# Two preactivated 5x5 convolutions: loading rows once, moving boundary rows to GpSimd, and filtering seven more chunks in columns

## The chip, the core and the metric

The kernel runs on one core of a Trainium2 chip. The metric is the device time of one execution in microseconds (us); lower is better. Five engines work side by side, each through its own instruction queue in order: TensorE (PE in the profile, with its weight loads as PEld), VectorE (DVE), ScalarE (ACT), GpSimd (POOL) and SyncE (SP), which here only issues transfers. GpSimd and ScalarE issue a few transfers too.

## The reference

```python
# x: (8, 32, 252, 252) float32, two weights of (32, 32, 5, 5)
x = x + conv(group_norm(x), w0)   # layer 1: 16 groups of 2 channels, eps 1e-5
x = x + conv(group_norm(x), w1)   # layer 2
# conv: 5x5 over all 32 channels, reflect padding of 2, written in the reference by FFT
```

The output has the shape of `x`. In the code the layers are `l = 0` and `l = 1`; this text calls them layer 1 and layer 2.

## The kernel before, in words

**Layout.** The image is split by the parity of its columns and rows into four phases. A phase's 32 channels take a quarter of the 128 partitions, so that one matmul of 128x128 handles all phases and channels at once, and the 5x5 filter becomes 3x3 on a plane of 126x126. An image and layer are worked through in 8 chunks `c` of 16 plane rows (`ROWS`), which are 4 tiles (`NT`) of 4 rows.

**Row filtering.** In the rows the kernel uses a fast filtering scheme with six points: of six input rows each tile makes six combinations (points 2, 4, 1, 3, 0 and 5), each is multiplied with its own transformed weights, and the six products are combined to four output rows. `transform` makes the combinations on VectorE: `row_pairs` (differences of rows two apart, into tile `v`), `row_quads` (L571, L572) and `last_rows` (L578, L579), both into tile `u12`, then `point2` (L587), `point4` (L591), `point1` (L597), `point3` (L594) and `points05` (L604). In layer 2 the row sums come from two transfers on GpSimd's queue instead of `row_pairs`: `v<-y` (L552) copies the rows, and L554 and L555 add the rows two further down as they land. The last rows of a chunk need the first rows of the next chunk; `last_rows` is the part that reads them.

**Products.** `conv` multiplies (L680): three matmuls for each point, one for each column tap, of 504 columns in layer 1 and 508 in layer 2. An fp32 product appears as two records in the profile. Points 2 and 4 go to `m`, 1 and 3 to `pairs`, 0 and 5 to `sums05` or `extra`.

**Column filtering.** For some chunks points 0 and 5 are also filtered fast in the columns. `by_columns` names them. Then `points05` writes into the buffer of `u12`, `columns` makes differences of neighbouring columns (L613 to L623), and `column_product` (L702) does four products of half the width for each of the two points, where the plain form does three of full width. The two middle ones share a buffer `extra`: the first pair is multiplied, ScalarE copies half of it (`seed_columns`, L706) as the start value of the second pair, and TensorE adds the second pair to it. `column_parts` (L787 to L789) puts the parts together.

**ScalarE** seeds `pairs` from `m` (L724, L726), evacuates `m` to `sd` (L732) and the first pair to `sd` (L739), writes rows 0 and 3 of the output (L768, L780, L778), copies reflected borders of `y` (L864 to L867, L862), interleaves the phases for the store (L917), and sums an image's pixels for the statistics (L231, L237, L855).

**Input.** `load` brings a chunk of `x` into `xs` (two buffers) from SyncE's queue: four transfers of 504 KB, one for each phase. Since the two column parities of a row differ only by a shift of one column, two transfers are enough where `once` is true: `even_columns` then copies 64 partitions to the other 64 with ScalarE (L159). `borders` (L148 to L154) fills the reflected columns on GpSimd. `parts` says in which pieces of rows a chunk is loaded.

**Order.** The program order of every engine is written by hand: `at(t, fn, ...)` puts a call into a table with a planned time, and the calls are emitted in the order of these times. After the first image, layer 1 of image `b + 1` and layer 2 of image `b` alternate chunk by chunk. A step is the stretch in which TensorE works on one chunk's points 2, 4, 1 and 3; in it, `transform` prepares the next chunk, and the chunk before gets its points 0 and 5. `begin(i)` is the planned start of step `i`: 10.2 us for the four points, and 5.1 for plain or 3.4 for column-filtered points 0 and 5.

## Time and profile before

| | |
|---|---|
| time, median of 3 runs | 1892.61 us (1891.02 to 1893.24) |
| the profiled execution | 1893.14 us, of which the span of the trace is 1891.4 |
| TensorE | 1851.5 us busy, 98% of the span |
| VectorE | 1698.0 us, 90% |
| ScalarE | 1401.1 us, 74% |
| GpSimd | 372.9 us, 20% |
| mean granted TensorE clock | 0.994 of full speed |
| transfers | 411.41 MB, 218 GB/s |

The span runs from the first instruction to the last. Busy times are sums over the span, so an engine that is busy for 74% on average may be full in one stretch and idle in another. TensorE's busy time comes from modelled ends of pipelined matmuls. "A <- B" in a list of waits says that A's engine was idle before A until B was done.

The program has 128 steps, 77 of them column-filtered. The planned lengths are close to those in the trace: a column-filtered step of layer 1 followed by a plain one of layer 2 takes 13.56 and 11.94 us between first matmuls.

### The profile page before, as it was taken

Reading aid. Unit: us, or ns where it says so; the run is one execution under the profiler, and the core shown is the slowest. Engines: PE = TensorE matmul, PEld = TensorE weight load, DVE = VectorE, ACT = ScalarE, POOL = GpSimd, SP = SyncE. Lnnn points to the kernel's source line nnn. Section 1 sums busy time; section 2 is a strip of 40 time slices with the busy share of each in tenths; the row PEclk is TensorE's granted clock in tenths of the full one; section 3 lists DMA queues with packets and bytes.
Section 4 is the critical chain, followed back from the end, with each engine's and each line's share of the span. In section 5 each row is a group of like instructions: output and inputs, shape, how many; then the busy total and the mean of one; then the engine's idle time right before and its main releaser. Section 6 shows DMA issues by size and latency. Waiting matters only on the chain.

```text
span 1891.4 us, 20043 instructions
## 1 busy us (share of the span) xinstructions
PE 1851.5 (98%) x5162; PEld 956.7 (51%) x5162; DVE 1698.0 (90%) x2972; ACT 1401.1 (74%) x2695; POOL 372.9 (20%) x733
## 2 busy tenths in 40 slices
PE   5999999999999999999999999999999999999997
PEld 4444455545555555544555455555555545554455
DVE  7987899999998999999899898999989999998685
ACT  5887678778777787778787687877787765565665
POOL 4543211120112210131111310113111131111210
PEclk8999999999999999999999999999999999999999
DMA  9887899999999999999999989999999978995785
GB/s 278 205 176 191 201 248 230 212 229 253 219 239 239 206 249 233 212 244 219 246 224 229 220 214 258 221 227 226 215 260 220 236 184 177 193 203 145 192 217 113
DMA packets 248627, 411.41 MB, mean 218 GB/s; under 512 B 19520, under 2 KB 215488, under 8 KB 238144
## 3 DMA queue, kind: packets, MB, share of 16 engines
q1 hardware_dynamic: 220384, 272.09, 61.8%
q0 software_dynamic: 27648, 135.28, 28.7%
q10 hardware_dynamic: 480, 2.77, 0.4%
q8 instruction: 41, 0.67, 0.2%
q14 instruction: 74, 0.61, 0.1%
HBM read 207.41 MB, written 67.39 MB: 145 GB/s over the span
## 4 chain that ended last, share of the span: by engine, by line
PE 76%; DVE 9%; DMA 8%; ACT 3%; issue 2%; POOL 1%; SPq 0%; DVEq 0%; ACTq 0%; POOLq 0%
PE m L680 27%; PE pairs L680 26%; PE sums L680 8%; PE sums L702 6%; PE extra L702 6%; DMA v<-y 4%; PE extra L680 4%; DMA st<-in_x_dram 1%; DMA xs<-in_x_dram 1%; DMA out_dram<-o 1%; DVE sd L743 1%; ACT o L917 1%; DMA v<-ytail 1%; DVE t L604 1%; POOL u L479 0%
## 5 line engine op out<-in xcount | busy, mean ns | idle before, releaser
L680 PE MATMUL pairs<-t,u 128*128 128x504 f32 (+2 forms) x1548 | 690.4, 585 | 2.7 <-ACT pairs L726 1.6
L680 PE MATMUL m<-t,u 128*128 128x508 f32 (+3 forms) x1560 | 675.2, 581 | 7.1 <-DVE t L591 2.6
L680 PEld LDWEIGHTS m<-t,u 128*128 128x128 f32 x1560 | 293.3, 189 | 325.6 <-issue 297.4
L680 PEld LDWEIGHTS pairs<-t,u 128*128 128x128 f32 x1548 | 289.2, 189 | 321.5 <-issue 295.6
L917 ACT COPY o<-y 64x508 f32<-64x508 f32 x496 | 327.2, 660 | 8.9 <-DMA out_dram<-o 0.2
L743 DVE SCALAR_TENSOR_TENSOR sd<-sd,pairs 128x504 f32<-128x504 f32 (+2 forms) x258 | 163.9, 670 | 19.2 <-PE pairs L680 16.0
L680 PE MATMUL sums<-t,u 128*128 128x508 f32 (+5 forms) x408 | 175.3, 578 | 0.0
L855 ACT ACTIVATE junk<-y,negk 128x1008 bf16<-128x1008 f32 (+1 forms) x144 | 147.4, 1024 | 30.6 <-PE extra L702 14.9
L726 ACT COPY pairs<-m 128x504 f32<-128x504 f32 (+1 forms) x129 | 72.5, 562 | 129.6 <-PE m L680 110.0
L732 ACT COPY sd<-m 128x504 f32<-128x504 f32 (+2 forms) x258 | 137.0, 583 | 32.0 <-DVE sums L789 24.7
L604 DVE SCALAR_TENSOR_TENSOR t<-v 128x1024 f32<-128x1024 f32 (+1 forms) x128 | 157.5, 1230 | 3.5 <-PE sums L680 3.5
L702 PE MATMUL extra<-sdiff,wc 128*128 128x252 f32 (+3 forms) x616 | 156.3, 375 | 3.3 <-ACT extra L706 2.6
L702 PEld LDWEIGHTS extra<-sdiff,wc 128*128 128x128 f32 x616 | 113.5, 188 | 89.6 <-issue 50.2
L591 DVE SCALAR_TENSOR_TENSOR t<-v 128x512 f32<-128x512 f32 (+2 forms) x129 | 89.7, 695 | 65.6 <-DMA v<-y 47.7
L702 PE MATMUL sums<-d,u 128*128 128x252 f32 (+3 forms) x616 | 142.3, 373 | 0.0
L562 DVE TENSOR_TENSOR v<-xs 128x1792 f32<-128x1792 f32 (+1 forms) x65 | 129.5, 1993 | 1.8 <-issue 0.7
L554 POOL DMA_DIRECT2D v<-y x64 | 55.2, 863 | 377.7 <-DMA v<-y 377.7
L702 PEld LDWEIGHTS sums<-d,u 128*128 128x128 f32 x616 | 115.3, 189 | 26.9 <-issue 11.8
L237 ACT ACTIVATE st<-st,negk 128x1134 f32<-128x1134 f32 x98 | 121.7, 1242 | 3.2
L148 POOL COPY xs<-xs 64x32 f32<-64x32 f32 (+3 forms) x74 | 34.1, 461 | 450.2 <-DMA xs<-in_x_dram 330.7
L680 PEld LDWEIGHTS sums<-t,u 128*128 128x128 f32 x408 | 75.9, 188 | 80.1 <-issue 77.2
L231 ACT ACTIVATE st<-st 128x1134 f32<-128x1134 f32 x98 | 112.2, 1145 | 4.0 <-DMA st<-in_x_dram 2.8
(171 smaller groups left out, 2424.7 us busy)
## 6 DMA issues: line engine op xcount, KB each, us to landing
xs<-in_x_dram SPq DMA_DIRECT2D x176, 504.0 KB, 12.6
v<-y POOLq DMA_DIRECT2D x64, 1032.0 KB, 5.7
st<-in_x_dram SPq DMA_DIRECT2D x111, 567.0 KB, 6.9
out_dram<-o SPq DMA_DIRECT2D x488, 126.0 KB, 5.7
v<-y POOLq DMA_DIRECT2D x64, 903.0 KB, 9.9
u<-ud SPq DMA_DIRECT2D x15, 1152.0 KB, 5.6
xs<-in_x_dram SPq DMA_DIRECT2D x30, 441.0 KB, 6.7
xs<-in_x_dram SPq DMA_DIRECT2D x28, 472.5 KB, 11.1
```

The lines of the kernel that those rows point to most:

```text
L231: A.activation(junk, src, AF.Identity, accum_out=acc[:, 0, i : i + 1])
L237: A.activation(junk, src, AF.Square, bias=negk, accum_out=acc[:, 1, i : i + 1])
L562: V.tensor_sub(v[:, r0:r1], t[:, r0 + 2 : r1 + 2], t[:, r0:r1])
L591: stt(ts[b, l, c][0][:, 1, j0:j1], vt[:, :, 1], -2.0, vt[:, :, 2], ALU.mult, ALU.add)
L604: stt(t, got["vt"][:, :, 0:2], 4.0 if l else -4.0, got["vt"][:, :, 2:4], ALU.mult, ALU.add)
L680: T.matmul(dst, u[:, k, 2 - i, :], rhs[:, j0 + i0 : j0 + i1, i : i + wo], start=(i == 0 and not add), stop=(i == 2), skip_group_check=add,)
L702: T.matmul(dst[:, 0, use], w, rhs[:, use], start=(i == 2), stop=True, skip_group_check=(i != 2))
L726: A.copy(dst, src)
L732: A.copy(got["sd"][:, 1 + e], m24[e][:, 0:n])
L743: stt(d, d, -2.0, pairs13[e][:, 0:n], ALU.mult, ALU.add)
L855: A.activation(dst, src, AF.Square, bias=negk, scale=1.0 if i else -1.0, accum_out=acc[:, 1, at_ : at_ + 1])
L917: copy(got["o", h][halves[s], 0:m, cp::2], got["y"][halves[cp], r : r + m, :])
```

## The change

Rows of layer 1 are loaded once in more chunks: in image 1 in chunks 0 to 6 instead of 0 to 2, and in images 2 to 7 in chunks 0, 1 and 3 to 6 instead of none. That makes 40 more chunks with two transfers in place of four and with one ScalarE copy of 64x2048 elements. For them, and for the other chunks from (1,3) on, the planned times of load, borders and copy are new.

`last_rows` runs on GpSimd in all chunks but those of image 0 in layer 1. What was one VectorE instruction (scale and add) is there a scaling and an addition. Its planned time is 1.1 us earlier, except in layer 1 of the first two images.

`by_columns` names chunks 1, 3, 4, 6 and 7 of layer 2 for images 0 to 5 (before: 1, 3, 5 and 7) and 1, 3 and 4 for image 6 (before: 1 and 3).

```diff
     def once(b: int, c: int) -> bool:
 
-        return c < (NCH - 1, 3)[b] if b < 2 else False
+        return c < NCH - 1 and (b < 2 or c != 2)
 
     def parts(b: int, c: int):
 
         if once(b, c):
+            if b > 1 or (b == 1 and c > 2):
+                return ((0, ROWS),)
             return ((0, 10), (10, 6)) if (b, c) == (0, 0) else ((0, 2), (2, 14))
...
             u2, (t, nxt) = got["u"][:, 1], source()
+            eng = V if b + l == 0 else G
+            f = 4.0 if l else -4.0
+            if eng is V:
+                stt(u2[:, NT - 1], t[:, ROWS - 2], f, nxt[:, 0], ALU.mult, ALU.add)
+            else:
+                G.tensor_scalar(u2[:, NT - 1], t[:, ROWS - 2], f, None, ALU.mult)
+                G.tensor_add(u2[:, NT - 1], u2[:, NT - 1], nxt[:, 0])
             if l == 0:
-                V.tensor_sub(got["v"][:, ROWS - 2 : ROWS], nxt[:, 0:2], t[:, ROWS - 2 : ROWS])
-            stt(u2[:, NT - 1], t[:, ROWS - 2], 4.0 if l else -4.0, nxt[:, 0], ALU.mult, ALU.add)
+                eng.tensor_sub(got["v"][:, ROWS - 2 : ROWS], nxt[:, 0:2], t[:, ROWS - 2 : ROWS])
...
-            for dt, fn in ((2, row_quads), (3.2, last_rows), (3.6, point2)):
+            for dt, fn in ((2, row_quads), (3.2 if l == 0 and b < 2 else 2.1, last_rows), (3.6, point2)):
                 at(t0 + dt, fn)
...
-        return c in {B - 1: (1, 2, 4, 5), B - 2: (1, 3)}.get(b, (1, 3, 5, 7))
+        return c in {B - 1: (1, 2, 4, 5), B - 2: (1, 3, 4)}.get(b, (1, 3, 4, 6, 7))
...
                 for part in parts(*inputs[k]):
-                    early = once(*inputs[k]) or nb == 0
-                    at(t0 + (14.0 if nb == 0 and part[0] == ROWS else 4.0 if early else 9.5), load, *inputs[k], *part)
-                    at(t1 + (0.2 if early else 9.0), borders, *inputs[k], *part)
-                    if once(*inputs[k]):
-                        kb, kc = inputs[k]
-                        t = 5.25 if part[0] == 0 and (kb, kc) != (1, 0) else 13.55 if kb else 8.5
-                        at(t1 + t, even_columns, *inputs[k], *part)
+                    kb, kc = inputs[k]
+                    if kb > 1 or (kb == 1 and kc > 2):
+                        at(t0 + (7.5 if once(kb, kc) else 9.5), load, kb, kc, *part)
+                        at(t1 + (5.1 if once(kb, kc) else 9.0), borders, kb, kc, *part)
+                        if once(kb, kc):
+                            at(t1 + 6.3, even_columns, kb, kc, *part)
+                    else:
+                        early = once(kb, kc) or nb == 0
+                        at(t0 + (14.0 if nb == 0 and part[0] == ROWS else 4.0 if early else 9.5), load, kb, kc, *part)
+                        at(t1 + (0.2 if early else 9.0), borders, kb, kc, *part)
+                        if once(kb, kc):
+                            t = 5.25 if part[0] == 0 and (kb, kc) != (1, 0) else 13.55 if kb else 8.5
+                            at(t1 + t, even_columns, kb, kc, *part)
```

Here `V` is VectorE, `G` GpSimd, `stt` a VectorE instruction that scales one operand and adds another. In the last part `t0` and `t1` are the planned starts of the current and the next step, and `inputs[k]` is the chunk of `x` two ahead of the one that is transformed.

## The prediction
> **What bounds the kernel now.** The profiled execution took 1893.14 us around a span of 1891.4; the three timed runs have median 1892.61, 0.5 below it. I read the page's engine totals, then the chain of waits, then TensorE's own waits.

> ```profile
> PE 1851.5 (98%) x5162; PEld 956.7 (51%) x5162; DVE 1698.0 (90%) x2972; ACT 1401.1 (74%) x2695; POOL 372.9 (20%) x733
> ...
> PE 76%; DVE 9%; DMA 8%; ACT 3%; issue 2%; POOL 1%; SPq 0%; DVEq 0%; ACTq 0%; POOLq 0%
> ```

> ```profile
> PE extra L702 <- ACT extra L706: 2.6, 9, 0.9
> ```

> TensorE has work for 98% of the span, and outside the head hardly waits for anyone (last line: us in total, times, longest): a matmul less is time less, and a TensorE wait more is time more. The other engines matter only where they come late for a matmul. So I looked at one step in the timeline: the layer 1 step (4,0,3), filtered in columns, which starts at 929.85 (us from the span's start, us taken).

> ```profile
> 929.85 5.23 PE L680 MATMUL m<-t,u 128*128 128x504 f32 x12
> ...
> 932.45 0.64 ACT L780 ACTIVATE y<-sums 128x504 f32<-128x504 f32 x1
> ...
> 933.20 0.69 DVE L758 TENSOR_TENSOR sums<-pairs,sd 128x508 f32<-128x508 f32 x1
> ...
> 935.60 1.07 ACT L732 COPY sd<-m 128x504 f32<-128x504 f32 x2
> 935.72 1.21 DVE L617 TENSOR_TENSOR d<-t 128x1008 f32<-128x1008 f32 x1
> ...
> 936.96 0.70 DVE L571 SCALAR_TENSOR_TENSOR u<-y 128x516 f32<-128x516 f32 x1
> ...
> 937.71 0.58 ACT L739 COPY sd<-pairs 128x504 f32<-128x504 f32 x1 [1.04 <-PE pairs L680]
> ...
> 939.35 0.57 ACT L706 ACTIVATE extra<-extra 128x504 f32<-128x504 f32 x1 [0.36 <-PE extra L702]
> ...
> 940.84 1.01 PE L702 MATMUL extra<-sdiff,wc 128*128 128x252 f32 x4
> ```

> In times from the step's start: ScalarE ends the two evacuations (L732) at 6.8, and the seed L706 at 10.07; the second half of the middle column products (L702) needs that seed and starts at 10.99, 0.92 later. VectorE ends the last column difference (L617) at 7.08, and only then starts layer 2's next row filter (L571, 7.11). That is a floor: L758 starts at 3.35, just after ScalarE's L780 ends at 3.24 (it frees `sums05`), and ScalarE works without a gap from the evacuations of the step before to there. Over all column-filtered layer 1 steps in which a layer 2 chunk's rows are filtered, L571 starts between 7.09 and 9.88, never earlier.

> [...] at 805.62 a border copy (L154, else 0.21) took 1.22 beside a 1.24 us L604. [...] Here 128x384 takes GpSimd 1.255 (L459) and VectorE 0.566 (L572), 2.2 times.

> **The change part by part.**

> *Column filtering in seven more chunks.* Each drops six row products and adds eight half-width ones. From the chain (start, us):

> ```profile
> 941.86 5.11 PE sums L680 x12
> ...
> 956.35 1.70 PE pairs L680 x4
> 958.05 0.86 PE extra L702 x4
> 958.91 1.72 PE sums L702 x8
> ```

> 5.11 - (2 x 0.86 + 1.72) = 1.67 us, seven times: **-11.7 us** on the path. It costs VectorE seven more operations, 4.8 us a chunk (2.8 in the differences, 2.0 in the parts, 34 us in all), and ScalarE 0.7; the same chunks' neighbours lose theirs in part (5 goes back to rows, 4 and 6 come).

> *Last rows on GpSimd.* VectorE loses L578 (0.43) and L579 (0.29) in 56 layer 1 chunks and L579 in 64 of layer 2: about 0.72 and 0.4 between starts, 66 us, more than the 34. GpSimd gets three and two operations instead. Its queue: the first `v<-y` DMA, then layer 1's last rows, the accumulating DMAs, layer 2's last rows, the borders. VectorE's point 2 waits for the last rows: about 0.3, 1.3 (worked out below) against the 1.08 of L571 and L572. What hides it is that point 2 now ends 0.76 or more before TensorE reads it, and VectorE gains time; without that cover it would be 0.3 x 64 = 19 us. At nothing.

> *Rows loaded once.* 40 chunks of 2 x 504 KB fewer, 40 of 411 MB. Transfers are hidden behind the matmuls: late ones make VectorE wait for `v<-y` (47.7 us in 17 waits), but of this TensorE feels 2.6. SP's queue issues 2 DMAs fewer a chunk (2.67 us for 4), and its wait for the buffer moves from VectorE's L579 to GpSimd's last rows, no later. At nothing. But 40 copies go to ScalarE. From 1792 elements (1.85) and 256 (0.43), 2048 elements take 0.926 ns an element more: 2.09, **2.11 with the gap**.

> *Where that copy stands.* In ScalarE's order it follows the evacuations and precedes L739, the four reflections and the seed. In 33 of the 40 cases this is a column-filtered layer 1 step like the one above. The copy waits for GpSimd's borders, since it reads the border columns. The borders now stand in GpSimd's queue behind layer 2's last rows, and these write the `u12` buffer, which in such a step holds the points 0 and 5 that L617 reads last. So what ran side by side becomes a chain: L617 -> last rows -> borders -> copy -> L739 -> reflections -> seed -> TensorE.

> GpSimd's share does not show before; the nearest rows (after the bar: busy us, mean ns of one):

> ```profile
> L479 POOL TENSOR_TENSOR u<-u,resid 32x64 f32<-32x64 f32 x180 | 82.2, 457 | 52.8 <-ACT u L511 41.9
> ...
> L148 POOL COPY xs<-xs 64x32 f32<-64x32 f32 x54 | 26.3, 487 | 400.1 <-DMA xs<-in_x_dram 282.5 <-DVE u L579 37.1 <-DVE t L587 23.8
> ...
> L154 POOL COPY xs<-xs 64x16 f32<-64x16 f32 x54 | 19.2, 355 | 0.0
> L153 POOL COPY xs<-xs 64x16 f32<-64x16 f32 x54 | 18.7, 346 | 351.5 <-DMA xs<-in_x_dram 334.9 <-DMA out_dram<-o 9.1 <-DMA xtail<-in_x_dram 7.5
> ...
> L459 POOL TENSOR_TENSOR uraw<-blocks 128x384 f32<-128x384 f32 x3 | 3.8, 1255 | 0.1
> ```

> The add at 128 elements lies between 457 (64) and 1255 (384): 0.62. The scaling, between 0.246 (128x16, L187) and 1.33 (384): 0.58. The borders: 0.49 + 0.35 + 0.36 less 0.12 of overlap, 1.07. Hand-overs 0.15. Together **2.4**[...]

> Sum from the step's start: 7.15 + 2.4 + 0.05, copy 2.11, L739 0.475, reflections 0.81, seed 0.575, 0.05 to TensorE: 13.62 against 10.99, a TensorE gap of **2.63**. Even with GpSimd at zero the copy would start at 7.15 and end the chain at 11.2, 0.2 late. Nothing gives the gap back: the next step starts later by as much, and ScalarE and VectorE still catch up on TensorE in it.

> 27 of these steps (c = 2, 3, 4, 6) cost 2.63: 71.0 us. In the six with c = 1 (images 2 to 7) L571 started at 9.2 to 9.65; VectorE's savings before it (0.72 + 0.1 + 0.72) bring it to 8.0, and the reflections have two more operations (0.6): 4.1 each, 24.5 us. The other seven copies lie in steps whose points 0 and 5 have another buffer, at least 16 us long, with a ScalarE gap of 3.1 us in (1,0,7): nothing, at worst 1 us each.

> 71.0 + 24.5 - 11.7 = **+84 us**; some 4 us of the present lags at c = 7 and 0 (a 21.70 us step beside one of 20.78, one of 13.92 beside 12.66) go as VectorE gets time: +80, 1973 on the profiled run, **1972** on the median.

> **The rivals.**
> 1. *The new chain holds TensorE up, about as priced*: 1972. With 1.6 for GpSimd the gaps are 1.8 and 3.2: 68 - 15 = +53, 1946; with 3.4, 3.6 and 5.1: 128 - 15 = +113, 2005. Chance 0.72.
> 2. *The same chain, but small*: the seed still comes late, yet by 1 us, because VectorE's columns or GpSimd's five operations come earlier: 33 - 12 = +21 to +45. Against it: the 7.09 floor. Chance 0.14.
> 3. *Faster*: the copy is absorbed and TensorE keeps the 11.7 us: 1881, with vanished lags 1876. ScalarE has the room: idle 1.4 before the seed and 0.92 of slack are 2.35 against 2.11 in an undisturbed step. It decides if the borders end before about 7.0, so the last rows would have to start by 4.6; for that VectorE must end L617 2.5 us earlier than it ever does. Chance 0.08.
> 4. *ScalarE becomes the bound*: it falls behind in layer 2's steps too, the pair seeds come late there (in (3,1,3) the seed ends 1.7 before its matmuls; 0.9 of that goes after a late seed, since ScalarE then stands 2.6 before the next step and not 3.5), another 1 us in 33 steps: above 2005. Chance 0.05.
> 5. *No difference*: gaps that just eat the 11.7 us, 0.35 in each step. Chance 0.01.

> That the change does not do what it says is excluded by its instruction order, which has all 40 copies, the moved rows and 84 column chunks instead of 77.

> **How the numbers follow.** A run of this kernel can tell about 0.2% (3.8 us) from no change. Slower: 0.72 + 0.14 + 0.05 = 0.91; same 0.01; faster 0.08. The likeliest case's own range is 1946 to 2005; towards rival 2 and a little beyond the top, 1918 to 2010 leaves out some 2 in 10 (the faster case, the smallest of rival 2, the largest of rival 4).

> **What would show it.** Right: TensorE waiting at the second `extra` products for ScalarE's seed some 33 times, 2 to 4 us each, 85 to 100 us in all; ScalarE waiting at the copy for GpSimd's last border, some 2.7 us each; layer 1 steps of 13.56 grown to about 16; L571 still at about 7.1; fewer `v<-y` waits of VectorE. Wrong: those waits under 0.4 us, borders that end before 7.0, or TensorE's new idle time at another place.

## The result, and the profile after

The changed kernel takes **2095.33 us** (median of 4 runs, 2079.05 to 2109.74) against 1892.60 of the kernel before on the same chip: a ratio of 1.107, interval 1.0988 to 1.1152. The forecast had the direction and the chain, but 1972 us and a range that ended at 2010. The profiled execution took 2093.39 us with a span of 2091.5.

The page's totals, and the chain that ended last by engine:

```profile
PE 1905.0 (91%) x5190; PEld 991.0 (47%) x5190; DVE 1733.8 (83%) x2845; ACT 1480.6 (71%) x2742; POOL 663.7 (32%) x1029
...
PE 21%; DVE 20%; ACT 7%; issue 4%; DMA 3%; POOL 3%; SPq 1%; DVEq 0%; ACTq 0%; POOLq 0%
```

TensorE falls from 98% to 91% of the span. The chain is followed back only to 866.8 us here, so its shares add up to 59% and can't be set against the 76% before. In the part that is followed, TensorE has 21 of 59 and VectorE 20: TensorE no longer sets the pace alone. Its busy time has grown by 53.5 us although it was given 11.7 us less to do. The list of waits (us in total, times, longest) says where it stands idle:

```profile
POOL u L584 <- DVE d L625: 372.2, 47, 14.9
...
ACT xs L159 <- POOL xs L151: 144.9, 42, 5.2
...
PE extra L710 <- ACT extra L714: 128.0, 41, 5.3
```

These three lines are the predicted chain from its start to its end (after the change L710, L714 and L625 are what were L702, L706 and L617): GpSimd's last rows wait for the column differences, ScalarE's copy for GpSimd's last border, TensorE's second pair for the seed. The last of the three was 2.6 us in 9 waits.

The timeline of the same step as in the prediction, (4,0,3), which now starts at 1030.90:

```profile
1030.90 5.23 PE L688 MATMUL m<-t,u 128*128 128x504 f32 x12
...
1036.73 1.20 DVE L625 TENSOR_TENSOR d<-t 128x1008 f32<-128x1008 f32 x1
...
1037.97 0.70 DVE L573 SCALAR_TENSOR_TENSOR u<-y 128x516 f32<-128x516 f32 x1
...
1038.10 0.97 POOL L584 TENSOR_SCALAR u<-y 128x129 f32<-128x129 f32 x1 [6.64 <-DVE d L625]
...
1039.15 0.41 POOL L585 TENSOR_TENSOR u<-u,y 128x129 f32<-128x129 f32 x1
...
1040.30 0.73 POOL L151 COPY xs<-xs 64x16 f32<-64x16 f32 x1
...
1041.06 2.00 ACT L159 COPY xs<-xs 64x2048 f32<-64x2048 f32 x1 [3.35 <-POOL xs L151]
...
1044.26 0.58 ACT L714 ACTIVATE extra<-extra 128x504 f32<-128x504 f32 x1
...
1044.89 1.35 PE L710 MATMUL extra<-sdiff,wc 128*128 128x252 f32 x4 [2.84 <-ACT extra L714]
...
1046.04 6.78 PE L688 MATMUL sums<-t,u 128*128 128x508 f32 x12
```

From the step's start: L573 at 7.07 (the floor of 7.1 held in this step; in (7,0,3) L573 started at 5.76), GpSimd from 7.20 to 10.13, copy from 10.16, TensorE at 13.99. Predicted were 9.55 for GpSimd's end and 13.62 for TensorE; the gap is 2.84 where 2.63 was worked out. But then the plain points 0 and 5 take 6.78 us, and they took 5.11. Busy time and granted clock by stretch (PEclk is the third value from the end) say why:

```profile
1030.90:1044.89 13.99, 11.15 (x29) 5.10 (x28) 9.65 (x15) 9.12 (x20) 3.40 (x6) 1.00 0.93 205
1044.89:1052.65 7.76, 7.76 (x16) 3.85 (x17) 4.77 (x10) 3.56 (x6) 0.63 (x1) 0.78 0.44 152
```

After the gap TensorE was granted half its clock for 3.41 us. Over the span the trace's clock records hold 157.1 us at half clock and 24.2 before; 133 us more at half speed are 66 us of work not done. The 200.1 us between the two spans are, then: TensorE idle 146.6 longer (39.9 to 186.5), half clock about 65, columns -11.7. Of the idle time 118 lie before second pairs in layer 1 steps, some 25 in layer 2's steps of chunk 7, and some 4 elsewhere.

### The profile page after: what moved, and what is told of

It reads as the page before. It is cut to its first block, busy times and chain, and to the rows that moved or that the text cites. A ratio compares the mean times of both kernels' runs of the same rounds, so it can differ in the third digit from the quotient of the medians.

```text
span 2091.5 us, 20253 instructions
## 1 busy us (share of the span) xinstructions
PE 1905.0 (91%) x5190; PEld 991.0 (47%) x5190; DVE 1733.8 (83%) x2845; ACT 1480.6 (71%) x2742; POOL 663.7 (32%) x1029
## 4 chain that ended last, share of the span: by engine, by line
PE 21%; DVE 20%; ACT 7%; issue 4%; DMA 3%; POOL 3%; SPq 1%; DVEq 0%; ACTq 0%; POOLq 0%
PE m L688 6%; PE pairs L688 6%; PE sums L688 5%; PE extra L710 2%; ACT xs L159 2%; DMA xs<-in_x_dram 2%; DVE v L564 2%; PE sums L710 2%; DVE sd L751 2%; POOL u L584 1%; DVE sdiff L621 1%; DVE sums L795 1%; DVE sdiff L622 1%; DVE d L625 1%; DVE sd L796 1%
## 5 line engine op out<-in xcount | busy, mean ns | idle before, releaser
L710 PE MATMUL extra<-sdiff,wc 128*128 128x252 f32 (+3 forms) x672 | 192.9, 412 | 128.0 <-ACT extra L714 128.0
L710 PEld LDWEIGHTS extra<-sdiff,wc 128*128 128x128 f32 x672 | 131.9, 204 | 231.0 <-ACT extra L714 169.6
L159 ACT COPY xs<-xs 64x2048 f32<-64x2048 f32 (+4 forms) x59 | 101.0, 1715 | 150.8 <-POOL xs L151 144.9
L584 POOL TENSOR_SCALAR u<-y 128x129 f32<-128x129 f32 x64 | 55.7, 870 | 379.2 <-DVE d L625 357.3
L584 POOL TENSOR_SCALAR u<-xs 128x128 f32<-128x128 f32 x56 | 93.5, 1669 | 246.5 <-ACT pairs L734 117.5
L710 PE MATMUL sums<-d,u 128*128 128x252 f32 (+3 forms) x672 | 166.5, 393 | 0.0
L688 PE MATMUL sums<-t,u 128*128 128x508 f32 (+5 forms) x324 | 157.7, 640 | 0.0
L710 PEld LDWEIGHTS sums<-d,u 128*128 128x128 f32 x672 | 133.4, 201 | 28.2 <-issue 7.3
L795 DVE TENSOR_TENSOR sums<-extra,sd 128x504 f32<-128x504 f32 (+1 forms) x84 | 57.8, 688 | 107.0 <-ACT y L776 93.0
L595 DVE TENSOR_TENSOR t<-u 128x512 f32<-128x512 f32 (+2 forms) x129 | 107.9, 836 | 35.5 <-POOL u L585 24.8
L564 DVE TENSOR_TENSOR v<-xs 128x1792 f32<-128x1792 f32 (+1 forms) x65 | 133.6, 2056 | 0.9 <-ACT xs L159 0.3
```

Source lines behind the costliest of these rows:

```text
L159: copy(t[64:128, :, 0:256:2], t[0:64, :, 1:256:2])
L564: V.tensor_sub(v[:, r0:r1], t[:, r0 + 2 : r1 + 2], t[:, r0:r1])
L584: G.tensor_scalar(u2[:, NT - 1], t[:, ROWS - 2], f, None, ALU.mult)
L595: V.tensor_sub(ts[b, l, c][0][:, 0, j0:j1], got["u"][:, 1, j0:j1], got["u"][:, 0, j0:j1])
L688: T.matmul(dst, u[:, k, 2 - i, :], rhs[:, j0 + i0 : j0 + i1, i : i + wo], start=(i == 0 and not add), stop=(i == 2), skip_group_check=add,)
L710: T.matmul(dst[:, 0, use], w, rhs[:, use], start=(i == 2), stop=True, skip_group_check=(i != 2))
```

## The experiments

All changes of time are against the kernel before in the same batch. "Alone" means on top of the kernel before.

### The three parts, alone and in pairs

**e1_columns**, the new list of chunks only:

```diff
-        return c in {B - 1: (1, 2, 4, 5), B - 2: (1, 3)}.get(b, (1, 3, 5, 7))
+        return c in {B - 1: (1, 2, 4, 5), B - 2: (1, 3, 4)}.get(b, (1, 3, 4, 6, 7))
```

> The kernel before with the seven more column-filtered chunks alone. Theory (the loss is the chain GpSimd last rows, borders, ScalarE copy, seed): the loss is absent, and 7 x 1.67 us of matmuls go: about 1881, up to 1890 if VectorE's 34 us more, without the relief of the moved rows, make some points late. Rival (VectorE becomes the bound by the added column operations): clearly above 1893, with TensorE waiting for t<-u, t<-v or sdiff.

1917.06 us, +24.0 (ratio 1.0133, 1.0105 to 1.0161). The saving does not arrive. TensorE's waits in e1 show for what:

```profile
PE m L342 <- DVE mv L332: 8.1, 5, 2.9
PE m L680 <- issue: 8.0, 5, 1.9
PE extra L702 <- ACT extra L706: 7.5, 10, 1.2
PE m L680 <- DVE t L591: 4.5, 2, 4.0
```

`mv` holds the moments of an image, made by VectorE in the layer 1 step of chunk 7. The five layer 2 steps (b,1,7) of images 1 to 5 hold 13.2 us of TensorE idle time, 2.1 before; the trace puts 5.3 of them down to ScalarE's seed and 6.4 to "issue", a wait for nothing that it shows. That VectorE is behind these two is not shown. In the whole trace TensorE is idle 23.2 us longer, and half clock adds some 12 us (47.8 us, 24.2 before); less the 11.7 saved this is about what the span has grown (1916.4, 1891.4 before).

**e2_gpsimd_rows**, `last_rows` on GpSimd only, with its planned time:

```diff
+                G.tensor_scalar(u2[:, NT - 1], t[:, ROWS - 2], f, None, ALU.mult)
+                G.tensor_add(u2[:, NT - 1], u2[:, NT - 1], nxt[:, 0])
...
-            for dt, fn in ((2, row_quads), (3.2, last_rows), (3.6, point2)):
+            for dt, fn in ((2, row_quads), (3.2 if l == 0 and b < 2 else 2.1, last_rows), (3.6, point2)):
```

> The kernel before with last_rows on GpSimd alone, planned 1.1 us earlier as in the change. Theory: no copy waits behind the borders, so 1886 to 1894; VectorE's slack grows. Rival (GpSimd's slow operations hold up VectorE's point 2, or the transfers v<-y behind them in GpSimd's queue, and so TensorE): 1910 or more, with TensorE waiting for VectorE.

1900.04 us, +7.0 (1.004, 1.0024 to 1.0056). VectorE has 176 instructions fewer, yet is busy for 1703.5 us and not less than the 1698.0 of before. The groups (busy us, mean ns of one) of the kernel before and of e2 show what it lost again:

```profile
L587 DVE TENSOR_TENSOR t<-u 128x512 f32<-128x512 f32 (+2 forms) x129 | 89.1, 691 | 14.1 <-PE m L680 1.6
...
L571 DVE SCALAR_TENSOR_TENSOR u<-xs 128x512 f32<-128x512 f32 (+1 forms) x65 | 44.6, 687 | 0.7 <-ACT xs L159 0.7
L571 DVE SCALAR_TENSOR_TENSOR u<-y 128x516 f32<-128x516 f32 x64 | 44.5, 696 | 1.7
```

```profile
L593 DVE TENSOR_TENSOR t<-u 128x512 f32<-128x512 f32 (+2 forms) x129 | 100.6, 780 | 37.7 <-POOL u L583 28.0 <-PE m L686 1.2 <-DVE u L572 0.5
...
L571 DVE SCALAR_TENSOR_TENSOR u<-xs 128x512 f32<-128x512 f32 (+1 forms) x65 | 61.2, 942 | 0.5 <-ACT xs L159 0.5
...
L572 DVE SCALAR_TENSOR_TENSOR u<-xs 128x384 f32<-128x384 f32 (+1 forms) x65 | 45.6, 701 | 0.0
L571 DVE SCALAR_TENSOR_TENSOR u<-y 128x516 f32<-128x516 f32 x64 | 44.7, 698 | 1.7
```

The row quads and point 2, which run while GpSimd takes the last rows, became longer, and mainly in layer 1 (`u<-xs`): 687 to 942 ns, 559 to 701 (L572) and 692 to 875 (the layer 1 part of point 2, now L593; 780 is the mean over both layers). In layer 2 (`u<-y`) L572 went from 556 to 634, while L571 and point 2 stayed at 696 to 698. The instructions taken off VectorE were 59 us long together and the others became some 50 us longer; since the records of neighbouring instructions overlap less than before, the busy time did not fall at all. Point 2 also waits 28.0 us for GpSimd.

**e3_once**, rows loaded once only, with all its planned times:

```diff
-        return c < (NCH - 1, 3)[b] if b < 2 else False
+        return c < NCH - 1 and (b < 2 or c != 2)
...
+                        at(t0 + (7.5 if once(kb, kc) else 9.5), load, kb, kc, *part)
+                        at(t1 + (5.1 if once(kb, kc) else 9.0), borders, kb, kc, *part)
+                        if once(kb, kc):
+                            at(t1 + 6.3, even_columns, kb, kc, *part)
```

> The changed kernel with last_rows on VectorE and the old column chunks: rows loaded once, with the new planned times, alone. Theory: borders have nothing before them in GpSimd's queue, so the copy starts when the evacuations end (6.8 to 8.3 after the step's start); in the steps c = 2, 3, 4 and 6 it fits or is at most 1 us late, in c = 1 about 2 us, after c = 7 some 2 us: 1900 to 1930. Rival (ScalarE is full, the 83 us of copies are the loss whatever they wait for): 2000 or more.

1958.99 us, +65.9 (1.0345, 1.0329 to 1.036), well beyond what was expected without GpSimd's rows. Its timeline around the step (4,0,6), which starts at 1048.64:

```profile
1043.93 0.30 DVE L581 SCALAR_TENSOR_TENSOR u<-xs,xs 128x128 f32<-128x128 f32 x1
...
1044.29 4.73 SPq L143 DMA_DIRECT2D xs<-in_x_dram  x5
...
1057.14 0.23 POOL L148 COPY xs<-xs 64x32 f32<-64x32 f32 x1 [11.85 <-DMA xs<-in_x_dram]
...
1057.46 0.67 POOL L151 COPY xs<-xs 64x16 f32<-64x16 f32 x1
...
1058.16 2.04 ACT L159 COPY xs<-xs 64x2048 f32<-64x2048 f32 x1 [2.71 <-DMA out_dram<-o]
...
1061.41 0.57 ACT L708 ACTIVATE extra<-extra 128x504 f32<-128x504 f32 x1
...
1062.03 1.12 PE L704 MATMUL extra<-sdiff,wc 128*128 128x252 f32 x4 [2.24 <-ACT extra L708]
```

`xs` has two buffers. The transfers start when VectorE has read the last rows out of the older one (L581), and the first border begins 12.8 us after that, 8.5 after the step's start. The copy starts 0.03 us after the last border (L151), whatever its bracket names: too late for a copy that stands ahead of the seed. The wait `POOL xs L148 <- DMA xs` has 443.9 us in 56 waits in e3.

This step is of the worst kind. It reads the first rows of the next image, in five transfers (x5), since the reflected rows are fetched apart. Of the 41 us that TensorE waits before second pairs in e3's layer 1 steps, 18 lie in the six such steps of chunk 6, and 13 in those of chunk 1. In chunks 2 and 3, with two transfers, the gap is 0 to 0.2 us in 12 of 14 steps.

The pairs came later, beside **f3_columns_gpsimd** (columns and GpSimd's rows, without loading once); the diffs are those above, two at a time.

> The kernel before with two of the three parts, the seven more chunks filtered in columns and the last rows on GpSimd, and with rows loaded as before. The prediction let the relief of VectorE by the second pay for the first; alone they cost 24 and 7 us. Theory: the relief is real on VectorE's queue, but GpSimd takes the rows late, so it pays for little: 1915 to 1930. If the relief pays in full as predicted: 1880 to 1890. If the two hinder each other (GpSimd's rows wait for a VectorE that the columns make later): above 1935.

1936.09 us, +42.3 (1.0233, 1.0208 to 1.0258): the two together cost 11 more than their sum, 1 us inside the range of the third case, in which they hinder each other.

> The changed kernel with the last rows on VectorE as before: rows loaded once with the copy ahead of the seed, and the seven more chunks in columns. GpSimd then has nothing ahead of the borders but its DMA issues. Alone the two parts cost 66 and 24 us. Theory: without the rows on GpSimd there is no chain through VectorE, and the two parts nearly add: 1970 to 2000. Rival: it is the columns' load that makes the copy late (VectorE, then ScalarE's evacuations behind it), and the excess of 106 us lies between these two: 2040 to 2090.

1970.93 us, +79.3 (1.041, 1.0388 to 1.0433): 11 less than the sum, as the theory had it and at the lower end of its range.

> The changed kernel with the old chunks in columns: rows loaded once with the copy ahead of the seed, and the last rows on GpSimd ahead of the borders, but not the seven more chunks. Alone the two parts cost 66 and 7 us. Theory: the prediction's chain, in which the borders stand behind GpSimd's last rows and these behind VectorE's row quads, needs just these two parts, so most of what the three cost beyond their sum (106 us) is between them: 2030 to 2070. Rival: they add, and the excess comes only with the columns' load on VectorE: 1960 to 1975.

2085.29 us, **+193.6** (1.1013, 1.0995 to 1.1031), even above what was expected. The wait for the seed in this kernel is that of the full change:

```profile
PE extra L710 <- ACT extra L714: 128.1, 41, 5.9
```

| parts | change of time, us |
|---|---|
| columns | +24.0 |
| GpSimd's rows | +7.0 |
| rows once | +65.9 |
| columns and GpSimd's rows | +42.3 |
| columns and rows once | +79.3 |
| GpSimd's rows and rows once | +193.6 |
| all three | +202.7 |

Loading once and GpSimd's rows cost 121 us more together than their sum. That is the chain, and it needs both: the copy gives ScalarE's seed a predecessor on GpSimd, and the rows give GpSimd a predecessor on VectorE. The 9 us that the seven chunks add to the two are within the scatter of the changed kernel (2079.05 to 2109.74), so they are not shown.

### Where the copy and the borders stand

**e4_borders_first**, the change with the borders ahead of the last rows in GpSimd's order:

```diff
-                        at(t1 + (5.1 if once(kb, kc) else 9.0), borders, kb, kc, *part)
+                        at(t1 + (4.9 if once(kb, kc) else 9.0), borders, kb, kc, *part)
```

> The whole change with one number altered: the borders of a chunk that is loaded once are planned at 4.9 instead of 5.1, so that they stand before layer 2's last rows in GpSimd's queue. Theory: the chain is cut; ScalarE no longer waits for the last border at the copy, the seed ends near 10.8 and TensorE's gaps at the second extra products fall from 2.8 to 5.3 us to under 0.5, the slow clock with them. What stays is some 2 us at each c = 7 and less at c = 1: 1883 to 1905. Rival (ScalarE is full): the gaps shrink by no more than the wait, about 1 us each, and the time stays above 2000.

2034.72 us, +141.6 (1.0745, 1.0701 to 1.0788): it gives back 61, not the 200 expected. Waits of GpSimd and TensorE, and the step (4,0,6) of e4, which starts at 1089.03:

```profile
POOL xs L148 <- DMA xs<-in_x_dram: 336.7, 44, 14.6
...
PE extra L710 <- ACT extra L714: 86.7, 39, 7.7
```

```profile
1097.45 0.23 POOL L148 COPY xs<-xs 64x32 f32<-64x32 f32 x1 [4.52 <-DMA xs<-in_x_dram]
...
1098.07 0.54 POOL L584 TENSOR_SCALAR u<-y 128x129 f32<-128x129 f32 x1
...
1099.14 0.70 DVE L595 TENSOR_TENSOR t<-u 128x516 f32<-128x516 f32 x1 [1.62 <-POOL u L585]
```

With the borders first, GpSimd waits for the landing (336.7 us, 109.7 in the change as it was) at 8.4 us into the step, as in e3, and now the last rows stand behind that wait, and point 2 behind them. One wait has taken the place of the other.

**f2_copy_late**, the change with the copy behind the seed:

```diff
-                            at(t1 + 6.3, even_columns, kb, kc, *part)
+                            at(t1 + 13.2, even_columns, kb, kc, *part)
```

> The changed kernel, with one time of the planner changed: the copy of the even columns, in the steps that read image 1's chunks from 3 on and images 2 to 7, at 13.2 us into the layer 1 step and no longer at 6.3. On ScalarE it then stands behind the seed, the piece sums and the squares, and ahead of the evacuation of the outer rows. Theory: the loss comes from the place of the copy ahead of the seed, where it passes GpSimd's lateness on; at the end of the step ScalarE has been seen idle for 2.7 us ahead of the outer rows, and the copy of 2.1 us fits there. The seed waits are gone, and with them the half clock: 1890 to 1930, TensorE idle under 70 us. Rival: ScalarE has no room for 40 copies of 2.1 us, wherever they stand: then the outer rows come late and the next step waits for them, and the time stays above 2000.

1944.63 us, +50.8 (1.0256, 1.0237 to 1.0274): **152 of the 203 us are gone** with one planned time, though the time is still 15 us above the top of the expected range. In f2's step (4,0,3), which starts at 956.84 and ends at 973.79, and in its list of TensorE's waits:

```profile
966.34 0.57 ACT L714 ACTIVATE extra<-extra 128x504 f32<-128x504 f32 x1 [0.37 <-PE extra L710]
...
970.57 2.09 ACT L159 COPY xs<-xs 64x2048 f32<-64x2048 f32 x1
```

```profile
PE m L344 <- DVE mv L334: 15.5, 6, 3.4
...
PE extra L710 <- ACT extra L714: 12.3, 15, 1.6
```

The seed starts at 9.50 and waits for TensorE only; the copy runs in the last 3.2 us of the step. ScalarE had room for it. What is left is about what columns and GpSimd's rows cost without it (50.8 against 42.3), and TensorE idles in the same place, the steps of chunk 7: 15.5 us in layer 1's and 23.8 in layer 2's in f2, 16.9 and 18.4 in f3, 1.1 and 4.9 before.

**f4_once_late**: e3 with the same edit.

> The kernel before with the one part, rows loaded once and copied, and with the copy at 13.2 us into the step and not at 6.3; alone with the copy at 6.3 that part took 1959. Theory: the 66 us are the copy's place ahead of the seed; behind the squares it is hidden: 1888 to 1902. Rival: ScalarE is full, or the transfers, which come in longer runs of rows, collide with others: 1935 to 1960.

1906.36 us, +12.6 (1.0068, 1.0055 to 1.008), 4 us above the range. 53 of e3's 66 us came from the copy's place. The rest lies in layer 2's plain steps behind a copy (12.46 us, 11.94 before) and in layer 1's of chunk 7 (21.7 in all six, 20.8 to 21.1 in five of them before).

### The half clock

**f1_filler**, the change with idle work for TensorE where it waits for the seed:

```diff
+        if l == 0 and by_columns(b, l, c) and (b > 1 or c > 2) and c not in (0, 5) and (b, c) != (B - 1, 6):
+            at(t0 + 11.1, warm, {1: 22, 6: 14}.get(c, 12), ident)
```

> The changed kernel, with extra products of the identity on TensorE put between the third point's products and the second pair of column products, in the layer 1 steps that hold a copy: 12 of about 0.22 us (2.6 us) in chunks 2, 3 and 4, 22 (4.8 us) in chunk 1, 14 (3.1 us) in chunk 6. They write a bank that the next step opens anew, and change no result. The chain from GpSimd to the seed is left as it is, so the seed comes as late as before; TensorE only does not stand idle meanwhile. Theory: some 65 of the 203 us lost are products run at half clock[...]. Then the half clock goes from most of these steps (about 110 of the 133 us at half clock lie there), and the time falls by about half of that, to 2030 to 2055. Rival: the half clock has another cause (load, or the time since the last one); then the time stays at 2085 to 2115 and the half clock stretches stay in number.

2062.32 us, +168.5 (1.0879, 1.0858 to 1.09), 33 faster than the change and 7 above the range. In f1's step (4,0,3):

```profile
1033.21 2.84 PE L1007 MATMUL m<-ident 128*128 128x128 f32 x24
...
1035.66 0.57 ACT L714 ACTIVATE extra<-extra 128x504 f32<-128x504 f32 x1
...
1036.29 1.12 PE L710 MATMUL extra<-sdiff,wc 128*128 128x252 f32 x4 [0.23 <-ACT extra L714]
...
1037.24 5.27 PE L688 MATMUL sums<-t,u 128*128 128x508 f32 x12
```

The seed is as late as before, but the next twelve products take 5.27 and not 6.78 us, and the step 20.13 and not 21.75. Between the first and the last step half clock falls from 133 to 48 us, and work that means nothing has made the kernel faster. In this kernel, then, the half clock came with the idle gaps. Of the 42 us that 85 us less at half clock are worth, 33 arrive; of the rest, 6 are second pairs that start later (124.1 us in all from the end of the products before the filler to the second pairs, against 118.4), and the others were not followed.

### Which chunks can be filtered in columns

Two other choices of seven more chunks, each alone and with one line changed in `by_columns`, and the first with GpSimd's rows as well:

```diff
-.get(b, (1, 3, 5, 7))
+.get(b, (1, 3, 4, 5, 7))      # h1_columns_5; with GpSimd's rows: h2_columns_5_gpsimd
+.get(b, (1, 2, 3, 5, 7))      # i3_columns_2
```

Both have (1, 3, 4) for image 6, as the change has.

> The kernel before with one line changed: chunks 1, 3, 4, 5 and 7 of layer 2 in columns, where the change has 1, 3, 4, 6 and 7 (as many chunks more, seven). Chunk 6 stays in rows. Theory: the 24 us that the columns cost alone lie around the last chunk's steps, where the column filtering of chunk 6 falls into the layer 1 step of chunk 7: its statistics (mv for the group mean, 8.1 us of waits) and the following step wait for VectorE. With chunk 5 in its place the two steps are as in the kernel before, and TensorE's saving of 7 times 1.67 us stands: 1880 to 1890, faster than both. Rival: VectorE can't take the columns' 34 us more in any chunk, three neighbours in columns least of all: 1900 to 1920, with waits in chunks 4 to 6.

1901.90 us, +10.2 (1.0053, 1.0037 to 1.0068). The step (b,1,7) is good again (1.1 us idle in five, 13.2 in e1), but the moments in the step before it still come late, and VectorE falls behind from chunk 4 on. TensorE's waits in h1:

```profile
PE m L342 <- DVE mv L332: 7.9, 6, 1.7
...
PE extra L702 <- DVE sdiff L614: 3.0, 10, 0.4
PE m L680 <- DVE t L587: 2.9, 3, 1.3
```

> The same with the last rows on GpSimd as in the change. Theory: GpSimd's rows only lengthen the wait of point 2 on VectorE, as they did alone (7 us) and with the other choice of chunks (19 us more): 1888 to 1905, slower than the same without them. Rival: they pay for VectorE's added work as the prediction had it: 1878 to 1886 and faster than without.

1914.29 us, +22.6 (1.0118, 1.0099 to 1.0136): 12 slower than without GpSimd's rows. They pay for nothing here either.

> The kernel before with one line changed: chunks 1, 2, 3, 5 and 7 of layer 2 in columns. The other two choices of seven more chunks cost 24 us (1, 3, 4, 6 and 7) and 10 us (1, 3, 4, 5 and 7) and both left VectorE late at the last chunk's statistics. Theory: VectorE has a debt after any two neighbouring chunks in columns and works it off in the steps without; with the three neighbours at 1 to 3 the waits come in chunks 3 and 4 (0.2 to 0.5 us a step), and the statistics at chunk 7 are on time as in the kernel before: 1886 to 1896, best of the three and no clear gain. Rival: VectorE's debt has no slack to be worked off in anywhere, and the statistics are late again: 1900 to 1915.

**1888.62 us, 3.4 faster than the kernel before** (18 runs; 0.9981, 0.9973 to 0.9989), and the fastest kernel of this study, though with 3.4 of the 11.7 us that the columns take from TensorE. TensorE's waits in i3:

```profile
PE extra L702 <- DVE sdiff L614: 3.4, 11, 0.4
...
PE m L342 <- DVE mv L332: 0.5, 1, 0.5
```

VectorE still has a debt after the neighbours (the five steps (b,1,3) took 70.9 us together, 68.3 before), but it is worked off by chunk 5, and the wait for the moments is 0.5 us and not 7.9. So where the same number of column chunks lies decides: VectorE comes late behind three neighbours, and the statistics wait only if these lie close ahead of them.

## Why the prediction was right and wrong

The step that failed is the price of a TensorE gap: "nothing gives the gap back" put it at its own length, and the half clock that stands behind it in the trace at nothing. That term came to about 65 us, half of the 133 us more at half clock. With it failed the relief of VectorE, which was to pay for the columns; the gaps themselves came out a quarter longer than priced.

- **The chain: right, by name and place.** Differences, GpSimd's last rows, borders, copy, seed, second pair: each stands in the waits above. Taking away either of two parts of it (the pairs) or its last link (f2) takes most of the loss away. VectorE's `v<-y` waits fell, as said, from 47.7 to 35.1 us.
- **The gap: somewhat small.** The ends of the range for GpSimd, 1.6 and 3.4, were the author's estimates. In (4,0,3) it took 2.93 us of the path and not 2.4: the borders took 1.52 where 1.07 was worked out and the scaling 0.97 for 0.58, the add 0.41 for 0.62. With c = 3 at 2.2 to 2.9, c = 2 and 4 at 3.2 to 3.3, c = 6 at 2.9 to 5.1 and c = 1 at 4.4 to 5.3, the term of 95.5 us (71.0 + 24.5) measured 118. GpSimd's share is not what differs, with 2.92 or 2.93 us in 27 of the 33 steps. In c = 2 and 4 the chain begins later (L573 at 7.5 in most steps), and in c = 1 too: 9.0 in four of the six where VectorE's savings were to bring it to 8.0. In c = 6 three first borders waited for the landing, until 11.3 to 11.8.
- **"Nothing gives the gap back": true, but a gap costs more than its length.** The half clock behind the gaps was left out of the sum, and is its largest missing term: about 65 us. f1 shows that it goes when the gaps are filled (133 us to 48), and the last section shows behind which idle time it stood.
- **"The other seven copies: nothing", and "some 4 us of the present lags at c = 7 and 0 go": the loss was looked for in the wrong place.** Layer 1's steps of chunk 7, with six of the copies, kept near nothing (2.1 us idle in all, 1.1 before). But layer 2's steps of chunk 7, where part of the 4 us was to go, lost some 25 more. Half of it is there with the columns alone (13.2 us in five steps in e1, 22.8 in the change). With the copies and GpSimd's rows but without the columns (g_once_gpsimd), the eight steps hold 8.2 us in all, 29.5 in the change and 4.9 before: most of it needs the columns.
- **"Columns -11.7 us on the path, VectorE's 34 us paid for by the last rows' 66": the payment failed.** TensorE's saving is real, but VectorE's relief on GpSimd is not: the instructions moved away were 59 us long and not 66, and nearly all of it came back, most of it as longer row quads and a longer point 2 (e2: L571 in layer 1 from 687 to 942 ns). The prediction priced longer operations on GpSimd, as in its 1.22 us border copy beside L604, and none on VectorE. And "34 us" was set against a total, where one stretch decides (h1 against i3).
- **"Rows loaded once: transfers hidden, at nothing": wrong.** Alone it cost 65.9. The floor "even with GpSimd at zero 0.2 late" held where the data are there in time, in most of e3's steps of chunks 2 and 3. In chunk 6, and at times in 1, 3 and 4, the landing is later than a copy ahead of the seed allows; before, nobody on the path waited for it. The floor was taken from VectorE's chain and did not ask when the data are there.
- **The sum.** Predicted on the profiled run: 95.5 - 11.7 - 4 = +80. Measured: 118 + 25 + 4 + 65 - 11.7 = +200.

Not settled: what the "issue" waits of layer 2's steps of chunk 7 are (9.2 us in the five steps in the change, none before).

## What to carry to other kernels

When an operation is put into an in-order queue, ask what stands behind it there, and move it behind what the bottleneck waits for: the same 40 copies cost about 66 us ahead of the seed and 13 behind it. Work moved from one engine to another pays only what the sum over both shows, and a saving counts only where the engine that pays for it has slack in that very stretch. Price a gap on TensorE at its length and at the half clock that the trace shows behind it: here 118 us of gaps in layer 1 stood beside 133 us more at half clock, worth about 65.

## What the runs showed of the hardware

```profile
496.09:499.51 3.42, 1.36 (x4) 0.31 (x2) 1.30 (x4) 2.62 (x4) 0.74 (x2) 1.00 0.07 23
499.51:502.92 3.41, 2.22 (x5) 1.85 (x6) 3.41 (x8) 3.35 (x8) 0.00 (x0) 0.50 0.00 0
...
752.09:755.51 3.42, 1.48 (x4) 0.38 (x2) 1.41 (x3) 2.50 (x3) 0.86 (x2) 1.00 0.07 28
755.51:758.92 3.41, 2.11 (x10) 1.89 (x11) 3.31 (x8) 3.35 (x9) 0.00 (x0) 1.00 0.00 0
```

- **GpSimd's last rows and VectorE's row filters took longer in some of the places where they ran beside each other.** In the change, L573 of layer 1 (L571 before) took 1.32 to 1.34 us in the 16 cases where GpSimd's subtraction (L587) overlapped it longest, 0.68 to 0.80 in the 34 with the scaling (L584), and 0.68 or 0.69 in the six of full size with nothing of GpSimd. In e2, one took 1.33 us at 987.75, where the subtraction ran from 985.91 to 988.53; at 960.66, with GpSimd's scaling at 3.24 us instead, it took 0.69. That scaling took 870 ns on average in layer 2 and 1669 in layer 1 of the change. In layer 1 it was 0.53 to 0.55 us in 21 of 56 cases, 2.16 to 2.18 in the 27 that ran beside the row differences (L564, some 2 us) and the first row quad (L573), and 2.9 to 3.2 in the seven that ran beside these and the second (L574). Layer 2 has no such row differences on VectorE. The cause of these lengths was not shown.
